# Gathering graph messages in tiles of 124 edges instead of 128

## The chip, the cores and the metric

The kernel runs on one core of one Trainium2 chip. The metric is the device time of the whole kernel in microseconds; lower is better. The kernel before takes 1381.88 us (median of two runs, 1380.68 and 1383.08).

Besides this time there is a profile of one execution. The profile's span, from its first to its last recorded instruction, is 1220.6 us. The device time is thus 161 us longer than the span. What lies in those 161 us the profile does not record.

## The reference

One layer of a graph network: each of 6250 nodes has 128 features, and 100000 edges of two types carry messages from a source node to a destination node. The edges come sorted by destination.

```
x    : [6250, 128] float32
src, dst, edge_type : [100000] int32, sorted by dst; type is 0 or 1

message(edge) = x[src] @ W_data.T + b_data          if type == 0
                x[src] @ W_control.T + b_control    otherwise
agg[n] = sum of message(edge) over the edges with dst == n
out    = layernorm(x + relu(agg + x @ W_self.T + b_self))
```

## The kernel before

Nodes are taken in 49 blocks of 128, and seven blocks make a group. The kernel has four stages.

1. It counts, for each block, how many destinations lie before it; that count is the place where the block's edges begin (line 96).
2. It multiplies all nodes with both message weights and stores the results in a table in DRAM, with row 2 * node + (type != 0) (lines 109 to 111).
3. For each block it loads a window of consecutive edges from the block's first one (line 123). KT = 18 tiles of P = 128 edges make a window of 2304 edges. An edge in the window that belongs to another block is to add nothing.
4. For each tile of a window, GpSimd starts an indirect DMA that gathers one table row of 512 bytes for each edge, each into a partition of its own (line 195). VectorE builds a one-hot matrix from the destinations (line 199). TensorE multiplies the two, which sums the messages by destination, and accumulates over the 18 tiles of the block (line 201). The residual and the layernorm follow.

The parts that matter here:

```
P = 128
KT = 18  # tiles of 128 edges in a block's window
WIN = KT * P
...
win = const.tile([P, NB, KT, 3], I32, name="win")
for b in range(NB):
    at = nc.values_load(first[0:1, b : b + 1], engines=(SP,), ...)
    nc.sync.dma_start(                                                   # line 123
        win[:, b, :, :], edges[ds(at, WIN), :].rearrange("(p k) c -> p k c", p=P)
    )
...
for g in range(NG):
    ...                             # idx, rel, low, inside of the whole group, on VectorE
    for j in range(GB):
        b = g * GB + j
        msg = deep.tile([P, KT, D], F32, name="msg")                     # 4 buffers
        hot = deep.tile([P, KT, P], F32, name="hot", bufs=3)
        agg = ps_a.tile([P, D], F32, name="agg")
        nc.tensor.matmul(agg, xt_sb[:, b, :], w_sb[:, 2 * D :], start=True, stop=False)
        for k in range(KT):
            nc.gpsimd.indirect_dma_start(                                # line 195
                out=msg[:, k, :], out_offset=None, in_=rows,
                in_offset=bass.IndirectOffsetOnAxis(ap=idx[:, j, k : k + 1], axis=0),
            )
            nc.vector.tensor_single_scalar(hot[:, k, :], slots, rel[:, j, k : k + 1],
                                           op=ALU.is_equal)              # line 199
            nc.tensor.matmul(agg, hot[:, k, :], msg[:, k, :],            # line 201
                             start=False, stop=k == KT - 1)
        residual(h[:, j, :], agg, b)
    norm_and_store(h, g)
```

At the end the kernel counts the edges that it matched. Only if one was missed does a loop over all edges do the sums again in any order. With the reference's inputs the fullest block has 2184 edges, fewer than the window holds, so the loop does not run.

Of the kernel before, what the change touches and what calls it, by code (L numbers as in the profile page):

```python
# [9 lines left out]
F32 = mybir.dt.float32  # L10
I32 = mybir.dt.int32
# [4 lines left out]
DRAM = bass.MemoryType.DRAM  # L16

P = 128
D = 128  # features
N = 6250  # nodes  # L20
E = 100000  # edges
NB = 49  # blocks of 128 nodes, the last one padded
NP = NB * P
GB = 7  # blocks in a group: one store, one set of norms
NG = NB // GB
KT = 18  # tiles of 128 edges in a block's window
WIN = KT * P
EC = 125  # edges are cut into 125 rows of 800
EPS = 1e-05


# [1 line left out]
def kernel(  # L33
    ctx: ExitStack,
    tc: tile.TileContext,
    x: bass.AP,  # [NP, D], zero rows behind N
    xt: bass.AP,  # [D, NP], its transpose
    edges: bass.AP,  # [E, 3]: source, destination, type
    w: bass.AP,  # [D, 3 * D]: data, control and self weights, transposed
    bias: bass.AP,  # [1, 3 * D]  # L40
    out: bass.AP,  # [N, D]
):
    """out = layernorm(x + relu(sum over in-edges of (W_type x_src + b_type) + W_self x + b_self))

    Both messages of each node go to a table in DRAM, at rows 2 * node + (type != 0). Edges come
    sorted by destination, so those of a block of 128 nodes lie behind one another: a window of
    WIN edges from the block's first one (found on the chip) is gathered from the table, 128 rows
    at a time, and summed by destination with one-hot matrices on the tensor engine. An edge
    outside its block matches no column there. The edges matched are counted; if any was missed
    (a block with more edges than its window, or edges in another order), a loop over all  # L50
    edges that takes them in any order does the sums again.
    """
    nc = tc.nc

    const = ctx.enter_context(tc.tile_pool(name="const", bufs=1))
    dram = ctx.enter_context(tc.tile_pool(name="dram", bufs=1, space=DRAM))
    work = ctx.enter_context(tc.tile_pool(name="work", bufs=2))
    deep = ctx.enter_context(tc.tile_pool(name="deep", bufs=4))
# [1 line left out]
    ps_a = ctx.enter_context(tc.tile_pool(name="ps_a", bufs=2, space=PSUM))  # L60
    ps_s = ctx.enter_context(tc.tile_pool(name="ps_s", bufs=1, space=PSUM))

# [1 line left out]
    e_all = const.tile([EC, E // EC, 3], I32, name="e_all")  # L64
    nc.gpsimd.dma_start(e_all, edges.rearrange("(p k) c -> p k c", p=EC))
    w_sb = const.tile([D, 3 * D], F32, name="w_sb")
# [9 lines left out]
    x_sb = const.tile([P, NB, D], F32, name="x_sb")  # L76
    x_rows = x.rearrange("(b p) f -> p b f", p=P)

# [1 line left out]
    ones = const.tile([P, 1], F32, name="ones")  # L80
    nc.vector.memset(ones, 1.0)
    slots = const.tile([P, P], F32, name="slots")
    nc.gpsimd.iota(slots, pattern=[[1, P]], base=0, channel_multiplier=0,
                   allow_small_or_imprecise_dtypes=True)
    base = const.tile([P, NB, KT], F32, name="base")
    nc.gpsimd.iota(base, pattern=[[P, NB], [0, KT]], base=0, channel_multiplier=0,
                   allow_small_or_imprecise_dtypes=True)

# [1 line left out]
    dst_f = const.tile([EC, E // EC], F32, name="dst_f")  # L90
    nc.vector.tensor_copy(dst_f, e_all[:, :, 1])  # L91
    before = const.tile([EC, NB], F32, name="before")
# [7 lines left out]
    first = const.tile([1, NB], I32, name="first")  # L100
    nc.vector.tensor_scalar_min(first, first_ps, float(E - WIN))

# [1 line left out]
    table = dram.tile([NP, 2 * D], F32, name="table")  # L104
    for g in range(NG):
        y = work.tile([P, GB, 2 * D], F32, name="y")
# [6 lines left out]
        )  # L113
    rows = table.rearrange("n (t f) -> (n t) f", t=2)

# [1 line left out]
    win = const.tile([P, NB, KT, 3], I32, name="win")  # L117
    for b in range(NB):
        at = nc.values_load(
            first[0:1, b : b + 1], engines=(SP,), min_val=0, max_val=E - WIN,  # L120
            skip_runtime_bounds_check_because="it counts edges and is held to E - WIN",
        )
        nc.sync.dma_start(
            win[:, b, :, :], edges[ds(at, WIN), :].rearrange("(p k) c -> p k c", p=P)
        )
    for g in range(NG):
        nc.scalar.dma_start(x_sb[:, g * GB : (g + 1) * GB, :], x_rows[:, g * GB : (g + 1) * GB, :])

    def table_rows(index, source, kind, shape):
        """index = 2 * source + (kind != 0)"""  # L130
        other = work.tile(shape, I32, name="other")
        nc.vector.tensor_single_scalar(other, kind, 0.0, op=ALU.not_equal)  # L132
        nc.vector.scalar_tensor_tensor(index, source, 2.0, other, op0=ALU.mult, op1=ALU.add)  # L133

    def residual(h, agg, b):
        """h = x + relu(agg + b_self)"""
        s = work.tile([P, D], F32, name="s")
        nc.vector.tensor_add(s, agg, bias_sb[:, 2 * D :])  # L138
        nc.vector.scalar_tensor_tensor(h, s, 0.0, x_sb[:, b, :], op0=ALU.max, op1=ALU.add)  # L139

    def norm_and_store(h, g):
        mv = work.tile([P, GB, 2], F32, name="mv")
        for j in range(GB):
            st = work.tile([P, 6], F32, name="st")
            nc.vector.bn_stats(st, h[:, j, :])  # L145
            nc.vector.bn_aggr(mv[:, j, :], st)  # L146
        # One step of Newton's method behind the table's square root: 1 / root is 2 / (s + v / s).
        v = work.tile([P, GB], F32, name="v")
        nc.vector.tensor_scalar_add(v, mv[:, :, 1], EPS)  # L149
        s0 = work.tile([P, GB], F32, name="s0")  # L150
        nc.scalar.activation(s0, v, AF.Sqrt)  # L151
        r0 = work.tile([P, GB], F32, name="r0")
        nc.vector.reciprocal(r0, s0)
        q = work.tile([P, GB], F32, name="q")
        nc.vector.tensor_mul(q, v, r0)
        nc.vector.tensor_add(q, q, s0)
        rstd = work.tile([P, GB], F32, name="rstd")
        nc.vector.reciprocal(rstd, q)
        nc.vector.tensor_scalar_mul(rstd, rstd, 2.0)
        o = work.tile([P, GB, D], F32, name="o")  # L160
        for j in range(GB):
            nc.vector.tensor_scalar(o[:, j, :], h[:, j, :], mv[:, j, 0:1], rstd[:, j : j + 1],  # L162
                                    op0=ALU.subtract, op1=ALU.mult)
        n0 = g * GB * P
        full = min(GB, (N - n0) // P)
        nc.sync.dma_start(
            out[n0 : n0 + full * P, :].rearrange("(b p) f -> p b f", p=P), o[:, :full, :]
        )
        if full < GB:
            n1 = n0 + full * P  # L170
            nc.sync.dma_start(out[n1:N, :], o[: N - n1, full, :])

# [1 line left out]
    counts = const.tile([P, NG], F32, name="counts")  # L174
    for g in range(NG):
        gs = slice(g * GB, (g + 1) * GB)
        shape = [P, GB, KT]
        idx = work.tile(shape, I32, name="idx")
        table_rows(idx, win[:, gs, :, 0], win[:, gs, :, 2], shape)
        rel = work.tile(shape, F32, name="rel")  # L180
        nc.vector.tensor_sub(rel, win[:, gs, :, 1], base[:, gs, :])  # L181
        low = work.tile(shape, F32, name="low")
        nc.vector.tensor_single_scalar(low, rel, float(P), op=ALU.is_lt)
        inside = work.tile(shape, F32, name="inside")
        nc.vector.scalar_tensor_tensor(inside, rel, 0.0, low, op0=ALU.is_ge, op1=ALU.mult,
                                       accum_out=counts[:, g : g + 1])
        h = work.tile([P, GB, D], F32, name="h")
        for j in range(GB):
            b = g * GB + j
            msg = deep.tile([P, KT, D], F32, name="msg")  # L190
            hot = deep.tile([P, KT, P], F32, name="hot", bufs=3)
            agg = ps_a.tile([P, D], F32, name="agg")
            nc.tensor.matmul(agg, xt_sb[:, b, :], w_sb[:, 2 * D :], start=True, stop=False)  # L193
            for k in range(KT):
                nc.gpsimd.indirect_dma_start(  # L195
                    out=msg[:, k, :], out_offset=None, in_=rows,
                    in_offset=bass.IndirectOffsetOnAxis(ap=idx[:, j, k : k + 1], axis=0),
                )
                nc.vector.tensor_single_scalar(hot[:, k, :], slots, rel[:, j, k : k + 1],  # L199
                                               op=ALU.is_equal)  # L200
                nc.tensor.matmul(agg, hot[:, k, :], msg[:, k, :], start=False, stop=k == KT - 1)  # L201
            residual(h[:, j, :], agg, b)
        norm_and_store(h, g)

# [1 line left out]
    total_ps = ps_s.tile([1, NG], F32, name="total_ps")  # L206
    nc.tensor.matmul(total_ps, ones, counts, start=True, stop=True)
    total_f = const.tile([1, 1], F32, name="total_f")
    nc.vector.tensor_reduce(total_f, total_ps, axis=mybir.AxisListType.X, op=ALU.add)
    total = const.tile([1, 1], I32, name="total")  # L210
# [1 line left out]
    matched = nc.values_load(total[0:1, 0:1])  # L212

    with tc.If(matched != E):
        # Rows behind N take what is not to be added: an edge whose destination an earlier edge of
        # its tile has already is in that edge's sum.
        sums = dram.tile([N + P, D], F32, name="sums")
        ident = const.tile([P, P], F32, name="ident")
        make_identity(nc, ident)
# [13 lines left out]
        with tc.For_i(0, E, EC) as i:  # L233
# [16 lines left out]
            n_again = work.tile([EC, 1], F32, name="n_again")  # L250
            nc.vector.scalar_tensor_tensor(again, same, 1.0, earlier[:EC, :EC], op0=ALU.mult,
                                           op1=ALU.mult, accum_out=n_again)
            # The destination, or a spare row where it came before.
            away = work.tile([EC, 1], F32, name="away")
            nc.vector.tensor_sub(away, spare[:EC], to)
            nc.vector.scalar_tensor_tensor(away, n_again, 0.0, away, op0=ALU.is_gt, op1=ALU.mult)
# [54 lines left out]
```

## Time and profile before

| What | Before |
|---|---|
| Device time, median | 1381.88 us |
| Span of the profile | 1220.6 us |
| GpSimd (POOL) busy | 843.7 us, 69% of the span |
| TensorE matmuls (PE) busy | 747.0 us, 61% |
| VectorE (DVE) busy | 305.0 us, 25% |
| DMA, mean rate | 63 GB/s |
| Indirect gathers | 882 = 49 blocks x 18 tiles |

The page gives, for each engine, the time it was busy, then the span in 40 slices of 30.5 us, then the DMA queues, then the chain of work that ended last, then the costliest groups of instructions. A group's row has its line in the kernel, its engine, its operation, the tiles that it writes and reads, how many there are, the total busy time and the mean of one in ns, and last the idle time of its engine just ahead of it with what ended that wait. The word "issue" stands for time in which an engine waited for nothing that the profile shows.

### The profile page before, as it was taken

How to read it: one execution, taken by the hardware profiler on the slowest of the kernel's cores; microseconds unless marked ns; L12 is line 12 of the kernel's file. 1: busy time of each engine (PE TensorE's matmuls, PEld its weight loads, DVE VectorE, ACT ScalarE, POOL GpSimd, SP SyncE). 2: the span in 40 equal slices, each digit the busy share in tenths (PEclk: the TensorE clock that was granted, in tenths of full speed). 3: DMA queues.
4: the chain of work that ended last, by engine and by line, in shares of the span. 5: the costliest groups of instructions: out<-in, count | busy, mean ns of one | idle time of the engine just before them, and what ended most of it. 6: DMA issues, size and time to landing. Idle time of an engine off the chain costs nothing.

```text
span 1220.6 us, 6620 instructions
## 1 busy us (share of the span) xinstructions
PE 747.0 (61%) x1964; PEld 478.7 (39%) x1964; DVE 305.0 (25%) x1362; ACT 2.7 (0%) x8; POOL 843.7 (69%) x889
## 2 busy tenths in 40 slices
PE   1094666666666666666666666666666666666664
PEld 0042444444444344444444444444444444444442
DVE  4982211221212312212213113113122112212101
ACT  0000000000000000000000000000000000000000
POOL 0005777777777777777777777777777777777774
PEclk9995555555555555555555555555555555555555
DMA  8063121122212211121222212222122211221121
GB/s 263 0 200 95 52 54 52 52 67 54 52 52 52 69 52 52 52 54 52 67 54 53 52 52 67 54 52 53 52 67 54 52 52 52 68 53 52 52 54 49
DMA packets 55893, 77.32 MB, mean 63 GB/s; under 512 B 21669, under 2 KB 40719, under 8 KB 55727
## 3 DMA queue, kind: packets, MB, share of 16 engines
q0 software_dynamic: 28368, 59.06, 18.6%
q1 hardware_dynamic: 14716, 8.16, 2.5%
q10 hardware_dynamic: 12768, 9.63, 2.4%
q8 instruction: 16, 0.26, 0.1%
q14 instruction: 25, 0.20, 0.1%
HBM read 67.17 MB, written 9.62 MB: 63 GB/s over the span
## 4 chain that ended last, share of the span: by engine, by line
POOL 63%; issue 23%; DMA 5%; DVE 5%; PE 2%; POOLq 0%; SPq 0%; DVEq 0%; ACT 0%; ACTq 0%
POOL msg L195 63%; DMA msg<-table,idx 4%; DVE less L96 4%; PE y_ps L109 2%; DMA xt_sb<-in_xt 1%; DVE hot L199 1%; DVE y L110 1%; PE agg L201 0%; DVE o L162 0%; POOLq L307 0%; SPq L67 0%; SPq L69 0%; POOLq L195 0%; PE first_ps L99 0%; DVE other L132 0%
## 5 line engine op out<-in xcount | busy, mean ns | idle before, releaser
L195 POOL DMA_INDIRECT msg<-table,idx x882 | 840.9, 953 | 362.6 <-issue 259.5
L201 PE MATMUL agg<-msg,hot 128*128 128x128 f32 x1764 | 695.2, 500 | 403.0 <-DMA msg<-table,idx 400.7
L201 PEld LDWEIGHTS agg<-msg,hot 128*128 128x128 f32 x1764 | 441.0, 311 | 656.5 <-DMA msg<-table,idx 656.2
L138 DVE TENSOR_TENSOR s<-agg,bias_sb 128x128 f32<-128x128 f32 x49 | 14.3, 292 | 790.4 <-PE agg L201 790.4
L199 DVE TENSOR_SCALAR hot<-slots,rel 128x128 f32<-128x128 f32 x882 | 189.0, 292 | 0.0
L96 DVE TENSOR_SCALAR_CACHE_REDUCE less<-dst_f 125x800 f32<-125x800 f32 x48 | 43.6, 980 | 0.0
L109 PE MATMUL y_ps<-w_sb,xt_sb 128*128 128x256 f32 x98 | 31.4, 449 | 18.5 <-DMA xt_sb<-in_xt 16.8
L193 PE MATMUL agg<-w_sb,xt_sb 128*128 128x128 f32 x98 | 31.2, 423 | 0.0
L109 PEld LDWEIGHTS y_ps<-w_sb,xt_sb 128*128 128x128 f32 x98 | 16.5, 207 | 31.9 <-issue 16.8
L193 PEld LDWEIGHTS agg<-w_sb,xt_sb 128*128 128x128 f32 x98 | 27.0, 333 | 0.6 <-DVE s L138 0.3
L99 PE MATMUL first_ps<-before,ones 125*1 125x49 f32 x2 | 0.3, 260 | 41.5 <-DVE less L96 41.5
L133 DVE SCALAR_TENSOR_TENSOR idx<-win,other 128x126 int32<-128x126 int32 x7 | 2.3, 324 | 88.0 <-DMA msg<-table,idx 88.0
L110 DVE TENSOR_TENSOR y<-y_ps,bias_sb 128x256 f32<-128x256 f32 x49 | 20.5, 424 | 5.0 <-PE y_ps L109 3.8
L99 PEld LDWEIGHTS first_ps<-before,ones 125*1 125x1 f32 x2 | 0.1, 80 | 41.8 <-DVE less L96 41.8
L139 DVE SCALAR_TENSOR_TENSOR h<-s,x_sb 128x128 f32<-128x128 f32 x49 | 14.5, 295 | 0.1
L145 DVE BATCH_NORM_STATS2 st<-h 128x6 f32<-128x128 f32 x49 | 13.7, 280 | 0.1
L162 DVE TENSOR_SCALAR o<-h,mv,rstd 128x128 f32<-128x128 f32 x49 | 13.5, 363 | 0.0
L146 DVE BATCH_NORM_AGGREGATE mv<-st 128x2 f32<-128x6 f32 x49 | 8.6, 176 | 0.9
L91 DVE CAST dst_f<-e_all 125x800 f32<-125x800 int32 x1 | 0.7, 693 | 15.5 <-DMA e_all<-in_edges 15.5
L151 ACT ACTIVATE s<-v 128x7 f32<-128x7 f32 x7 | 1.5, 208 | 1115.5 <-DVE v L149 1115.5
L96 DVE DVE_READ_ACCUMULATOR less<-dst_f 125x1 f32 x48 | 3.9, 82 | 0.0
L181 DVE TENSOR_TENSOR rel<-win,base 128x126 f32<-128x126 int32 x7 | 2.1, 305 | 0.0
(25 smaller groups left out, 19.2 us busy)
## 6 DMA issues: line engine op xcount, KB each, us to landing
msg<-table,idx POOLq DMA_INDIRECT x882, 2.5
table<-y ACTq DMA_DIRECT2D x7, 896.0 KB, 4.2
x_sb<-in_x ACTq DMA_DIRECT2D x7, 448.0 KB, 14.6
xt_sb<-in_xt SPq DMA_DIRECT2D x7, 448.0 KB, 10.4
out<-o SPq DMA_DIRECT2D x6, 448.0 KB, 3.0
win<-in_edges SPq DMA_DIRECT2D x49, 27.0 KB, 1.9
e_all<-in_edges POOLq DMA_DIRECT2D x1, 1171.9 KB, 15.2
out<-o SPq DMA_DIRECT2D x1, 384.0 KB, 3.4
```

What stands on the lines that cost most here:

```text
L96: nc.vector.tensor_scalar(less, dst_f, float(b * P), None, op0=ALU.is_lt, op1=ALU.add, accum_out=before[:, b : b + 1])
L109: nc.tensor.matmul(y_ps, xt_sb[:, g * GB + j, :], w_sb[:, : 2 * D], start=True, stop=True)
L110: nc.vector.tensor_add(y[:, j, :], y_ps, bias_sb[:, : 2 * D])
L138: nc.vector.tensor_add(s, agg, bias_sb[:, 2 * D :])
L139: nc.vector.scalar_tensor_tensor(h, s, 0.0, x_sb[:, b, :], op0=ALU.max, op1=ALU.add)
L145: nc.vector.bn_stats(st, h[:, j, :])
L146: nc.vector.bn_aggr(mv[:, j, :], st)
L162: nc.vector.tensor_scalar(o[:, j, :], h[:, j, :], mv[:, j, 0:1], rstd[:, j : j + 1], op0=ALU.subtract, op1=ALU.mult)
L193: nc.tensor.matmul(agg, xt_sb[:, b, :], w_sb[:, 2 * D :], start=True, stop=False)
L195: nc.gpsimd.indirect_dma_start(out=msg[:, k, :], out_offset=None, in_=rows, in_offset=bass.IndirectOffsetOnAxis(ap=idx[:, j, k : k + 1], a ...
L199: nc.vector.tensor_single_scalar(hot[:, k, :], slots, rel[:, j, k : k + 1], op=ALU.is_equal)
L201: nc.tensor.matmul(agg, hot[:, k, :], msg[:, k, :], start=False, stop=k == KT - 1)
```

## The change

A tile has R = 124 edges instead of 128. There are still 18 tiles to a window, so a window has 2232 edges instead of 2304, and the tiles `win`, `idx`, `rel`, `low`, `inside`, `msg` and `hot` have 124 partitions instead of 128. The sums of a block still go to 128 destinations. The fullest block's 2184 edges still fit into a window.

It is for the way in which an indirect gather is shared among the DMA engines[...].

The comments are also taken out of the file; line numbers in the part that matters are kept within one of the old ones. The core of the diff:

```diff
-KT = 18  # tiles of 128 edges in a block's window
-WIN = KT * P
+KT = 18
+R = 124
+WIN = KT * R
...
-    win = const.tile([P, NB, KT, 3], I32, name="win")
+    win = const.tile([R, NB, KT, 3], I32, name="win")
...
-            win[:, b, :, :], edges[ds(at, WIN), :].rearrange("(p k) c -> p k c", p=P)
+            win[:, b, :, :], edges[ds(at, WIN), :].rearrange("(p k) c -> p k c", p=R)
...
-        shape = [P, GB, KT]
+        shape = [R, GB, KT]
...
-        nc.vector.tensor_sub(rel, win[:, gs, :, 1], base[:, gs, :])
+        nc.vector.tensor_sub(rel, win[:, gs, :, 1], base[:R, gs, :])
...
-                                       accum_out=counts[:, g : g + 1])
+                                       accum_out=counts[:R, g : g + 1])
...
-            msg = deep.tile([P, KT, D], F32, name="msg")
-            hot = deep.tile([P, KT, P], F32, name="hot", bufs=3)
+            msg = deep.tile([R, KT, D], F32, name="msg")
+            hot = deep.tile([R, KT, P], F32, name="hot", bufs=3)
...
-                nc.vector.tensor_single_scalar(hot[:, k, :], slots, rel[:, j, k : k + 1],
+                nc.vector.tensor_single_scalar(hot[:, k, :], slots[:R], rel[:, j, k : k + 1],
                                                op=ALU.is_equal)
...
-    nc.tensor.matmul(total_ps, ones, counts, start=True, stop=True)
+    nc.tensor.matmul(total_ps, ones[:R], counts[:R], start=True, stop=True)
```

## The prediction

> **What bounds the kernel now.** I start with the page's chain of work that ended last, because it says which engine sets the end. The columns are shares of the span.
>
> ```profile
> POOL 63%; issue 23%; DMA 5%; DVE 5%; PE 2%; POOLq 0%; SPq 0%; DVEq 0%; ACT 0%; ACTq 0%
> POOL msg L195 63%; DMA msg<-table,idx 4%; DVE less L96 4%; PE y_ps L109 2%; DMA xt_sb<-in_xt 1%; DVE hot L199 1%; DVE y L110 1%; PE agg L201 0%; DVE o L162 0%; POOLq L307 0%; SPq L67 0%; SPq L69 0%; POOLq L195 0%; PE first_ps L99 0%; DVE other L132 0%
> ```
>
> Work of GpSimd on the gathers and the "issue" time between them are 86% of the chain. Next come the costliest groups of instructions.
>
> ```profile
> L195 POOL DMA_INDIRECT msg<-table,idx x882 | 840.9, 953 | 362.6 <-issue 259.5
> L201 PE MATMUL agg<-msg,hot 128*128 128x128 f32 x1764 | 695.2, 500 | 403.0 <-DMA msg<-table,idx 400.7
> L201 PEld LDWEIGHTS agg<-msg,hot 128*128 128x128 f32 x1764 | 441.0, 311 | 656.5 <-DMA msg<-table,idx 656.2
> L199 DVE TENSOR_SCALAR hot<-slots,rel 128x128 f32<-128x128 f32 x882 | 189.0, 292 | 0.0
> ```
>
> One gather occupies GpSimd for 953 ns. TensorE, the second busiest, waits 401 us in total for gathered rows: it follows GpSimd. To see whether GpSimd itself waits for anything I look at the timeline of the middle of the run (start, duration, what, and in brackets the idle time ahead and what ended it).
>
> ```profile
> 635.30 0.95 POOL L195 DMA_INDIRECT msg<-table,idx  x1 [0.30 <-issue]
> 635.39 0.50 PEld L201 LDWEIGHTS agg<-msg,hot 128*128 128x128 f32 x2 [0.81 <-DMA msg<-table,idx]
> 635.40 0.79 PE L201 MATMUL agg<-msg,hot 128*128 128x128 f32 x2 [0.52 <-DMA msg<-table,idx]
> 636.55 0.95 POOL L195 DMA_INDIRECT msg<-table,idx  x1 [0.30 <-issue]
> ```
>
> GpSimd works 0.95 us, pauses 0.30 us, and begins the next gather 1.25 us after the last. No semaphore ends the pause. The gathers run from 98 us (the first start that the trace gives for the line) to 1207.6 us (the last one's end): 1109.5 us for 882, or 1.258 us each. They are 91% of the span, and the rest of the program follows their pace: everything depends on how long GpSimd takes over one gather.
>
> Last, the DMA side, from the page's queues (packets, MB, share of 16 engines' span) and its list of issues (count, KB, us to landing).
>
> ```profile
> q0 software_dynamic: 28368, 59.06, 18.6%
> ...
> msg<-table,idx POOLq DMA_INDIRECT x882, 2.5
> ```
>
> The queue that GpSimd feeds keeps 16 engines busy for only 18.6% of the span. The DMA engines don't bound the kernel.
>
> [...] 28368 packets less the 144 that I leave to the other GpSimd load make 28224 = 882 x 32, which is 16 packets of data and 16 completions to a gather. [...] Here 8 rows x 512 bytes are just 4096, [...] which fits the 32. [...] the bar is 0.95 us, the landing is at 2.5 us. [...]
>
> **The change part by part.**
>
> *Fewer rows to a gather.* 128 to 124, or 3.1% fewer. If all 953 ns were spent row by row, this saves 953 x 4/128 = 30 ns, and over 882 gathers 26 us. This is the upper bound of this part.
>
> *Fewer shares.* Twelve of the 16 data shares go; the 16 completions stay. If all 953 ns went to the 32 pieces and nothing to rows, 12/32 of it would go: 357 ns, 315 us in all. This is an upper bound too. If instead the work goes by packets, then 31 rows in packets of 8 are 4 packets to an engine and again 16 to a gather, and nothing is saved.
>
> *The split that I choose.* The only other DMA that GpSimd starts is the plain load of the edges, 125 rows, 698 ns by the group of line 65. It has nearly as many rows and no indices. I therefore put the difference, 953 - 698 = 255 ns, down to the indices, row by row. The 698 ns I divide in three equal parts, for want of anything in the profile that divides them: 233 ns fixed, 233 by rows, 233 by shares and completions. Rows: (255 + 233) x 4/128 = 15 ns. Shares: 233 x 12/32 = 87 ns. Sum 102 ns to a gather, 882 x 102 ns = 90 us, all on the path that sets the end. This is an estimate; the equal thirds are a choice.
>
> *The 0.30 us pause.* It is between any two gathers, and I take it as unchanged.
>
> *Data on four engines.* Queue 0 was busy 0.186 x 16 x 1220.6 = 3632 engine-us; over 882 gathers at most 4.1 to a gather or 0.257 us to an engine for 8 rows and a completion, so at most 0.032 us for a row. 31 rows would then take 1.0 us on one engine, and a gather lands 0.74 us later, at some 3.2 us. [...] Hidden, because four buffers of 18 gathers lie ahead of TensorE. Only the very last gather's delay, under 1 us, reaches the end.
>
> *TensorE and VectorE.* Matrices with 124 rows instead of 128 stream the same 128 columns, so no saving in time is counted. Two pairs of matmuls back to back took 1.31 us at 626.02 us in the timeline, one alone 0.80: a further pair costs 0.51 us, well under the coming pace of 1.15 us. VectorE needs 0.21 us (189.0 us / 882) for each one-hot matrix. Neither becomes the bound.
>
> *The window loads on SP.* [...] The first group's indices start at 71.8 us, while the first gather waits until 98.1 us for the table; later groups have far more slack. At most 1 us is lost.
>
> *The sum.* 1381.9 - 90 + about 2 = 1294 us. Since one rival below costs time and one gives only the rows' part, I put the point at 1300 us.
>
> **The rivals.**
>
> *Rows or packets are all that counts.* [...] Then only up to 26 us go: 1356 to 1378 us. For it: the number of packets may stay at 32, and the plain 125-row load is not dramatically cheaper. Against it: nothing in the trace; the kernel has no other gather of another size.
>
> *Shares are nearly everything.* The saving nears 315 us: 1070 to 1180 us. [...] Against it: the completions for all engines remain, and the 0.30 us pause is untouched.
>
> *A slower path for the odd size.* 128 rows on 16 engines may be the well-trodden case, and 31 rows to an engine, with partial packets, may take more work per row. If a gather takes 10% longer, 95 ns x 882 = 84 us are lost: 1466 us. Nothing in the profile speaks for or against it.
>
> *The same four engines every time.* [...] four engines must take 1.0 us of rows every 1.15 us: 87% busy. The landing would grow and GpSimd might wait for space. The pace would be held near 1.0 to 1.25 us, so the gain would shrink rather than turn to a loss.
>
> **Range and chances.** The row and packet rival gives the upper part, the shares rival the lower one. I take 1160 to 1405 us for 8 in 10: it holds everything from three fifths of the full shares saving or so, (1381.9 - 1160) / (315 + 26) = 65%, up to a loss of 23 us. The limits of 2% are 1354 and 1410 us. Faster by over 2% gets 0.60, for it needs only 28 us or 32 ns a gather, which rows alone just miss and any real cost of shares brings. Within 2% gets 0.24, slower 0.16 for the odd-size path.
>
> **What would show it.** The group of line 195: its mean falls from 953 to about 850 ns if the thirds are right, to 923 or more if rows alone count, below 700 if shares are nearly everything, and rises over 953 on a slower path. The pause ahead of it stays 0.30 us. Queue 0's packets per gather tell how 31 rows are cut: 32 if in packets of 8, 20 if one packet holds an engine's share. The landing goes from 2.5 to about 3.2 us[...]. If GpSimd's wait for gathers in flight appears in place of "issue", the engines have become the bound. What would make the prediction wrong is above all the division into thirds. A second risk lies in the 161 us between span and device time, which I take as fixed: were they a stretch of the same gathers, the saving would be an eighth larger.

## The result, and the profile after

The changed kernel takes **1522.88 us** (median of 1522.2 and 1523.56) against 1381.88 us: ratio **1.102**, 95% interval 1.0988 to 1.1052. Beside the kernel before on another chip, where that one takes 1220.12 us, the ratio is **1.252** (1.2496 to 1.2538); the changed kernel hardly differs there, 1527.24 us. Why there are two ratios is taken up with the experiments. In both the change costs time, and it was predicted to save some, with 1300 us as the point.

The profile's span is 1521.5 us after 1220.6. First the chain of work that ended last, in shares of the span by engine.

```profile
POOL 65%; issue 19%; DMA 9%; DVE 3%; SPq 2%; PE 2%; POOLq 0%; DVEq 0%; ACT 0%; ACTq 0%
```

The chain is made of the same things as before, GpSimd's gathers and the pauses between them: 84% where it was 86%. No new wait has taken their place. Next the costliest groups (busy us, mean ns of one, idle time ahead and what ended it).

```profile
L196 POOL DMA_INDIRECT msg<-table,idx x882 | 1137.0, 1289 | 366.6 <-issue 256.4
L202 PE MATMUL agg<-msg,hot 124*128 124x128 f32 x1764 | 700.7, 501 | 696.1 <-DMA msg<-table,idx 695.9
...
L200 DVE TENSOR_SCALAR hot<-slots,rel 124x128 f32<-124x128 f32 x882 | 235.0, 398 | 0.0
```

One gather now takes 1289 ns of GpSimd instead of 953, though it fetches four rows fewer. The pauses are as they were (256.4 us in total after 259.5). TensorE computes as long as before, 501 ns a matmul after 500, and waits longer for rows: 696 us instead of 401. The gathers' busy time alone has grown by 1137.0 - 840.9 = 296 us, and the span by 301.

The DMA queue that GpSimd feeds (packets, MB, share of 16 engines' span) shows more packets:

```profile
q0 software_dynamic: 70704, 58.57, 16.7%
```

(70704 - 144) / 882 = **80 packets a gather**, where there were 32, with fewer bytes moved. The packet records of the trace, sorted by size, tell what they are:

| Bytes of a packet | Number in the trace | A gather | What it fits |
|---|---|---|---|
| 4096 | 10584 | 12 | 8 rows of 512 bytes: 3 in each of 4 lists |
| 3584 | 3528 | 4 | 7 rows: 1 in each of 4 lists |
| 32 | 31752 | 36 | 8 pieces of 4 bytes: 3 in each of 12 lists |
| 28 | 10584 | 12 | 7 pieces of 4 bytes: 1 in each of 12 lists |
| 4 | 14131 | 16 | 16 completions |

The packets of 4 bytes are taken for completions because the trace has as many of them, over all queues, as semaphore events that come from DMAs: 14810. A packet's record has its queue and size and not its DMA engine. The counts fit sixteen lists of 31 entries, each cut into packets of 8, 8, 8 and 7: four lists of rows, as I had assumed of 124 = 4 x 31, and twelve of pieces of 4 bytes. These pieces, 12 x 31 = 372 to a gather, are called **fillers** here; what they are for the trace does not say. The trace of the kernel before has 14112 packets of 4096 bytes, 16 to a gather, and none of 32 or 28 bytes: sixteen lists of 8 rows. So there are still sixteen lists, and by these counts every list has become 31 entries long instead of 8.

### The profile page after: what moved, and what is told of

It is laid out like the page before. It is cut to its first block, busy times and chain, and to the rows that moved or that the text cites. A ratio compares the mean times of both kernels' runs of the same rounds, so it can differ in the third digit from the quotient of the medians.

```text
span 1521.5 us, 6620 instructions
## 1 busy us (share of the span) xinstructions
PE 753.5 (50%) x1964; PEld 479.7 (32%) x1964; DVE 354.4 (23%) x1362; ACT 2.7 (0%) x8; POOL 1139.9 (75%) x889
## 3 DMA queue, kind: packets, MB, share of 16 engines
q0 software_dynamic: 70704, 58.57, 16.7%
## 4 chain that ended last, share of the span: by engine, by line
POOL 65%; issue 19%; DMA 9%; DVE 3%; SPq 2%; PE 2%; POOLq 0%; DVEq 0%; ACT 0%; ACTq 0%
POOL msg L196 65%; DMA msg<-table,idx 7%; DVE less L97 3%; PE agg L202 2%; SPq L120 1%; DMA xt_sb<-in_xt 1%; SPq L124 1%; DMA win<-in_edges 0%; POOLq L308 0%; DVE o L163 0%; PE y_ps L110 0%; DVE y L111 0%; SPq L70 0%; SPq L68 0%; DVE st L146 0%
## 5 line engine op out<-in xcount | busy, mean ns | idle before, releaser
L196 POOL DMA_INDIRECT msg<-table,idx x882 | 1137.0, 1289 | 366.6 <-issue 256.4
L202 PE MATMUL agg<-msg,hot 124*128 124x128 f32 x1764 | 700.7, 501 | 696.1 <-DMA msg<-table,idx 695.9
L202 PEld LDWEIGHTS agg<-msg,hot 124*128 124x128 f32 x1764 | 441.2, 310 | 955.5 <-DMA msg<-table,idx 955.4
L200 DVE TENSOR_SCALAR hot<-slots,rel 124x128 f32<-124x128 f32 x882 | 235.0, 398 | 0.0
L163 DVE TENSOR_SCALAR o<-h,mv,rstd 128x128 f32<-128x128 f32 x49 | 14.6, 419 | 0.0
L147 DVE BATCH_NORM_AGGREGATE mv<-st 128x2 f32<-128x6 f32 x49 | 12.3, 250 | 0.9
L157 DVE TENSOR_TENSOR q<-q,s 128x7 f32<-128x7 f32 x7 | 3.3, 466 | 0.0
```

Source lines behind the costliest of these rows:

```text
L196: nc.gpsimd.indirect_dma_start(out=msg[:, k, :], out_offset=None, in_=rows, in_offset=bass.IndirectOffsetOnAxis(ap=idx[:, j, k : k + 1], a ...
L200: nc.vector.tensor_single_scalar(hot[:, k, :], slots[:R], rel[:, j, k : k + 1], op=ALU.is_equal)
```

## The experiments

**The theories.** Theory A: a gather costs GpSimd a fixed part and a step for each row of the longest list; 124 rows make 31 steps, 128 rows make 8. Theory B: any gather with rows in fewer than 16 lists pays a fixed penalty. Theory C: the packets of a list count, 4 instead of 1. Theory E: the number of fillers counts. How other numbers of rows are divided is an assumption of mine: into as many lists of equal length as possible, up to 16. The expectations say "engine" for what is a list here. Packets were counted for 128, 124 and 127 rows alone, so for the rest the time of a gather is the test.

**The kernel before again (no edit).**

> The kernel before, run again on the same chip as the next three, to have its profile and its device time side by side: the first profile had a span of 1220.6 us where the device time was 1381.88 us, while the changed kernel has 1521.5 and 1522.88 us. If the gap is part of the program outside the recorded span, the span is again about 161 us shorter than the device time. If instead the gathers run at two different paces, 953 ns in one execution and about 181 ns more, (1381.88 - 1220.6) / 882 gathers, in another, then span and device time of one and the same execution agree within a few us, as they do for the changed kernel.

Measured: 1221.69 us in the median of 20 executions, and 1221.64 us for the kernel before in 23 others beside it. The span of the profiled one is 1220.2 us at a device time of 1222.37. So span and device time differ by 2 us in one and the same execution. The 161 us that the prediction took for a fixed part of the program are none.

**126, 125 and 120 rows.** The edits, on the changed kernel:

```diff
-R = 124
+R = 126        # or 125; or 120 with KT = 19
```

> Tiles of 126 rows, 18 to a window: [...] Theory A, rows to an engine: [...] a gather costs a fixed part and a step for each row to an engine. From 953 ns at 8 rows and 1289 ns at 31 rows: 14.6 ns a step, 836 ns fixed; 9 rows give 968 ns. Theory B, a fixed penalty for every gather that does not use all 16 engines: 1289 ns. Theory C, a cost for each packet to an engine, (1289 - 953) / 3 = 112 ns for each beyond the first: 2 packets, 1065 ns. In every theory the pause of 0.30 us stays.

> Tiles of 125 rows, 18 to a window: [...] Theory A, rows to an engine: 836 + 25 x 14.6 = 1201 ns. Theory B, a fixed penalty: 1289 ns. Theory C, packets to an engine: 4 packets as with 124 rows, 1289 ns. [...] 16 x 5 = 80 packets a gather on GpSimd's queue, as with 124.

> Tiles of 120 rows, 19 to a window, so that 2280 edges still cover the fullest block: 931 gathers instead of 882. [...] Theory A: 953 ns, as with 128 rows, because the rows to an engine are the same. Theory B: 1289 ns. Theory C: 953 ns. Under A and C the time rises over the kernel before by 49 gathers of 1.26 us, 62 us of span. 32 packets a gather[...].

Measured, from the costliest groups of the three profiles, in this order:

```profile
L196 POOL DMA_INDIRECT msg<-table,idx x882 | 879.7, 997 | 366.0 <-issue 255.7
```
```profile
L196 POOL DMA_INDIRECT msg<-table,idx x882 | 1063.4, 1206 | 365.8 <-issue 261.5
```
```profile
L196 POOL DMA_INDIRECT msg<-table,idx x931 | 917.3, 985 | 383.1 <-issue 270.4
```

| Rows | Lists x rows, assumed | Gather, ns | A | B | C | Time, us | Ratio to the kernel before |
|---|---|---|---|---|---|---|---|
| 126 | 14 x 9 | 997 | 968 | 1289 | 1065 | 1264.90 | 1.0354 (1.0337 to 1.0372) |
| 125 | 5 x 25 | 1206 | 1201 | 1289 | 1289 | 1450.07 | 1.1869 (1.1849 to 1.1889) |
| 120 | 15 x 8 | 985 | 953 | 1289 | 953 | 1318.67 | 1.0792 (1.0774 to 1.0810) |

B falls: a gather of 126 rows takes 997 ns and not 1289. C falls too: 125 and 124 rows would both have four packets to a list and differ by 83 ns, and 126 rows with two packets take hardly more than 120 with one. A is near everywhere, but 29 to 32 ns low at 126 and 120. A small fixed part for rows in fewer than 16 lists has to be added. With it 120 rows cost 49 more gathers of 1.29 us, 63 us, and 882 x 32 ns, 28 us: 91 of the 97 us measured. The first gather also starts 4.8 us later (103.9 after 99.1 us).

**Nineteen sizes side by side.** The edit, on the kernel before, 12 gathers of each size n ahead of its end:

```diff
+    got = deep.tile([P, KT, D], F32, name="msg")
+    for k in range(12):
+        nc.gpsimd.indirect_dma_start(out=got[:n, k, :], out_offset=None, in_=rows,
+            in_offset=bass.IndirectOffsetOnAxis(ap=idx[:n, 0, k : k + 1], axis=0))
```

> The kernel before with 228 more gathers ahead of its end, 12 of each of 19 sizes, into a buffer that nothing reads. Theory A, a step for each row of the engine that has most, whoever fills the others, with about 35 ns more when fewer than 16 engines have rows: 16, 32, 48, 64, 80, 96, 112, 128 rows (1 to 8 to an engine) rise by 13.5 ns from size to size, from 850 to 944 ns; 31, 62, 93 and 124 rows (31 rows each to 1, 2, 3, 4 engines) all take the same 1287 ns; 15 rows 885, 120 rows 979, 126 rows 992, 100 rows (10 each to 10 engines) 1006, 125 rows 1208, 61 rows on one engine 1695, 127 rows on one engine 2586 ns. Theory E, the fillers are what costs (0.85 ns each) and rows cost nothing: all sizes that use 16 engines take 944 ns alike; 31 rows take 82 ns more than 124, because their fillers are 465 against 372. The rows theory of the prediction, a cost for each row gathered: 31 rows are far cheaper than 124.

The groups by line, GpSimd alone; each size has a line of its own. These ten are, from above and divided as assumed, 127 rows in one list, 61 in one, then 124, 93, 62 and 31 rows, all in lists of 31, then 120 rows in 15 lists, 128 in 16, 15 in 15 and 16 in 16.

```profile
L262 POOL DMA_INDIRECT msg<-table,idx x12 | 30.5, 2542 | 3.7 <-issue 3.7
L253 POOL DMA_INDIRECT msg<-table,idx x12 | 19.9, 1658 | 3.7 <-issue 3.7
L241 POOL DMA_INDIRECT msg<-table,idx x12 | 15.4, 1284 | 3.7 <-issue 3.7
L247 POOL DMA_INDIRECT msg<-table,idx x12 | 15.3, 1272 | 3.7 <-issue 3.7
L250 POOL DMA_INDIRECT msg<-table,idx x12 | 15.1, 1260 | 3.7 <-issue 3.7
L256 POOL DMA_INDIRECT msg<-table,idx x12 | 15.1, 1259 | 3.7 <-issue 3.7
...
L235 POOL DMA_INDIRECT msg<-table,idx x12 | 11.7, 972 | 3.7 <-issue 3.7
L208 POOL DMA_INDIRECT msg<-table,idx x12 | 11.3, 943 | 3.7 <-issue 3.7
...
L259 POOL DMA_INDIRECT msg<-table,idx x12 | 10.4, 865 | 3.7 <-issue 3.7
...
L229 POOL DMA_INDIRECT msg<-table,idx x12 | 10.1, 841 | 3.7 <-issue 3.7
```

This is the run that tells the theories apart. A gather of 31 rows takes as long as one of 124, within 25 ns, as theory A has it with 31 steps for both. So the rows gathered cost nearly nothing, (1284 - 1259) / 93 = 0.27 ns each, and what counts is the longest list. From 31 to 127 rows in one list a step is (2542 - 1259) / 96 = 13.4 ns; in 16 lists, from 1 to 8 rows in each, (943 - 841) / 7 = 14.6 ns. Theory E falls twice: 31 rows, with more fillers by its own count (465 after 372), are not dearer than 124, and from 16 to 128 rows, sizes without a filler by that count, the time rises all the same. The nine sizes not shown, the multiples of 16 between and 100, 125 and 126 rows, follow the assumed division too: the first take 863 to 926 ns, the last three, with lists of 10, 25 and 9 rows, 992, 1191 and 980 ns. The extra for rows in fewer than 16 lists shows in neighbours with equal lists: 15 rows 865 ns against 16 rows 841, 120 rows 972 against 128 rows 943. It is 24 to 29 ns.

The 341 ns more of 124 rows (1284 - 943) are thus 29 ns extra for rows in fewer than 16 lists (972 - 943) and 312 ns for 23 steps more (1284 - 972), 13.6 ns each. One part of theory A stays open. With the fillers all sixteen lists are equally long by the packet counts, so a step more is sixteen entries more. Whether a step is work on sixteen lists side by side, or on one entry after another at some 13.6 / 16 = 0.85 ns each, these runs don't tell.

**All rows in one list.** The edit is R = 127.

> Tiles of 127 rows: [...] Theory A: 871 + 127 x 13.5 = 2586 ns a gather, with the pause 2.89 us, span 112 + 882 x 2.89 = 2660 us. Packets: 16 engines x (16 of data or filler + 1 completion) = 272 a gather. Theory B, a fixed penalty for fewer than 16 engines, as with 124 rows: 1289 ns, span 1520 us. The engine's own work, 16 packets of 4096 bytes at 0.16 us, is 2.5 us, so a gather lands at 5 us or more; if the engines are taken in turn this stays hidden, and if it were always the same engine it would set a pace of about 2.5 us, still under GpSimd's 2.89.

Measured: 2657.48 us, ratio 2.178 (2.1736 to 2.1824). The group and the queue:

```profile
q0 software_dynamic: 240048, 65.33, 15.4%
...
L196 POOL DMA_INDIRECT msg<-table,idx x882 | 2243.3, 2543 | 392.0 <-issue 386.5
```

The time came within 3 us of theory A's, but in part by luck: the gather is 43 ns shorter, 38 us in all, while the first one starts at 127.6 us, some 28 us later than in the kernel before (99.1). (240048 - 144) / 882 is 272 packets, as expected. The data packets of 4096 bytes took 0.23 us each in the mean of the packet records. Fifteen of them and one of 3584 bytes, one after another, are 3.6 us, more than the 2.85 us from one gather to the next; yet GpSimd never waited for a transfer, and a third of the data packets start while another is still under way. A gather lands 7.8 us after its issue in the median, so several are in flight at once; on which DMA engines their packets go is not shown.

**The changed kernel again, and one part of it undone.** In the second kernel the windows, indices, one-hot matrices and matmuls keep 124 rows, and only the gather goes back to 128; nothing reads the last four rows.

> The changed kernel again, beside the kernel before on one chip. The kernel before took 1221.6 us in 43 runs beside the last experiments, in keeping with its profile (1220.6) and not with its first two times (1381.88). If those two times are the odd ones, the changed kernel takes 1522 us again and the ratio is about 1.246: (1289 - 953) ns x 882 = 296 us more. If the pace of a gather changes from chip to chip, both kernels' times differ from 1221.6 and 1522.

Measured: 1527.24 us against 1220.12, ratio 1.2517 (1.2496 to 1.2538), the gather 1293 ns. As expected, this is a chip of the first kind, on which the kernel before takes 1220 to 1222 us; on the second kind it takes 1376 to 1384.

```diff
-        idx = work.tile(shape, I32, name="idx")
-        table_rows(idx, ...)
+        idx = work.tile([P, GB, KT], I32, name="idx")
+        nc.vector.memset(idx, 0)
+        table_rows(idx[:R], ...)
...
-            msg = deep.tile([R, KT, D], F32, name="msg")
+            msg = deep.tile([P, KT, D], F32, name="msg")
...
-                nc.tensor.matmul(agg, hot[:, k, :], msg[:, k, :], ...)
+                nc.tensor.matmul(agg, hot[:, k, :], msg[:R, k, :], ...)
```

> The changed kernel with one part undone: windows, indices, one-hot matrices and matmuls keep their 124 rows, but each gather fetches 128 rows, the last four of which (row 0 of the table) nothing reads. Only the way the gather is shared changes back, to 16 engines with 8 rows each. Theory A: 944 to 953 ns a gather again and 1222 us, within 5 us of the kernel before, so that the whole 307 us between 1220 and 1527 lie in the shape of the gather. Rival: a part of the loss comes from the other uses of 124 rows (window loads on four engines, VectorE and TensorE on 124 partitions); then a part of it remains, and the time lies clearly over 1225 us.

Measured: 1379.44 us, ratio 1.002, but on a chip where the kernel before takes 1376.43. The gathers are at 949 ns again, as theory A has it:

```profile
L197 POOL DMA_INDIRECT msg<-table,idx x882 | 837.1, 949 | 503.7 <-issue 252.0
```

Yet 882 x 1.25 us and the 112 us around them make 1215. The timeline of GpSimd shows where the rest is (start, duration, what, idle time ahead and what ended it):

```profile
627.75 0.94 POOL L197 DMA_INDIRECT msg<-table,idx  x1 [0.30 <-issue]
629.00 0.94 POOL L197 DMA_INDIRECT msg<-table,idx  x1 [0.30 <-issue]
...
636.15 0.94 POOL L197 DMA_INDIRECT msg<-table,idx  x1 [6.21 <-remote]
```

GpSimd stands still for 6 us. By the gathers' start times this happens 22 times, always at the first gather of a block, where it needs one of the four message buffers, and costs 138 us together. On this chip the buffers are not emptied in time, and GpSimd runs out of them.

> The last kernel again. There its gathers took 949 ns as theory A has it, but on that chip both it and the kernel before took 1376 to 1379 us instead of 1221, with TensorE's work in bursts 51 us apart and GpSimd waiting some 6 us in each: something other than the gathers set the pace, so the times could not separate the theories. On a chip where the kernel before takes about 1221 us this one takes 1222 to 1226 us under theory A; under the rival (a part of the loss in the other uses of 124 rows) clearly more. On a chip like the last one, about 1379 us again.

> The changed kernel a third time. On a chip where the kernel before takes 1221 us: 1523 to 1527 us, ratio 1.25. On a chip where the kernel before takes about 1376 us because TensorE sets the pace at (1376 - 112) / 1862 = 0.68 us a matmul of the main stage, or 1.43 us a tile, the changed kernel's GpSimd, at 1.59 us a tile, is the slower of the two and still takes about 1525 us: ratio 1.10 to 1.11, as in the first comparison. The rival, that such a chip is slower in everything by 13%, gives 1720 us there and a ratio of 1.25.

> The kernel with windows of two blocks again. On a chip where the kernel before takes 1221 us: 1166 us, ratio 0.955. On a chip where TensorE sets the pace at 0.68 us a matmul it has 3206 of them in the main stage instead of 1862, and takes 112 + 3206 x 0.68 = 2290 us, ratio 1.66; then it beats the kernel before only where TensorE is free to keep up.

The first two of these three, on one chip of that kind, against 1376.43 us for the kernel before: gathers of 128 rows 1378.91 us, ratio 1.0022 (1.0014 to 1.0029); the changed kernel 1522.62 us, ratio 1.1068 (1.1042 to 1.1093). The latter is the ratio of the first comparison. It is smaller because the kernel before is held up there, not because the change costs less: the changed kernel's gathers come 1.59 us apart and leave its consumers more time, GpSimd has no stall over 1 us in its trace, and it runs at the same pace on both kinds. Undoing the gather alone takes back 143.7 of the 146.2 us that the change costs on this chip.

> The changed kernel with gathers of 128 rows, once more. Where the kernel before takes about 1221 us: 1222 to 1226 us if the whole loss lies in how a gather is shared (theory A), clearly more if a part lies in the other uses of 124 rows. Where the kernel before takes about 1376 us: 1379 us, which tells nothing new.

> The changed kernel with gathers of 128 rows, for a chip on which the kernel before takes about 1221 us: 1222 to 1226 us if the whole loss lies in how a gather is shared (theory A), clearly more if a part lies in the other uses of 124 rows. Where the kernel before takes about 1376 us: about 1379 us, as three times already.

Both met that kind again and repeat the result: 1379.78 against 1376.38 us and 1386.24 against 1383.61, ratios 1.0023 and 1.0018. The time of this kernel where the kernel before takes 1221 us has therefore not been measured; the length of its gathers has.

**What holds the kernel before on those chips.** Every second matmul of the tiles is left out, and with it the sums of half of the edges:

```diff
-                nc.tensor.matmul(agg, hot[:, k, :], msg[:, k, :], ...)
+                if k % 2 == 1:
+                    nc.tensor.matmul(agg, hot[:, k, :], msg[:, k, :], ...)
```

> The kernel before with every second matmul of the tiles left out (the sums of half of the edges are missing from its output; all gathers and one-hot matrices remain). Where the kernel before takes about 1221 us, GpSimd sets the pace and nothing changes: 1221 us, ratio 1.00. Where it takes about 1376 us: if TensorE sets the pace there, the time falls to about 1221 us, ratio 0.887; if something else there makes GpSimd or the transfers wait, it stays at 1376 us.

Measured: 1359.08 us against 1376.38, ratio 0.9886 (0.9867 to 0.9904). This is near the second outcome: half of TensorE's tile work gone brings 17 us of some 155. So, against what I had thought, the amount of matmuls is not what sets the pace there. The trace of the kernel with gathers of 128 rows (1379.44 us) agrees: TensorE is busy for 24% of its span and idle for some 35 us at a time. From 601.6 to 636.3 us, for one, it does nothing, while the gathers' data and completion packets keep coming, 16 of each to a gather, until GpSimd stalls. The cause stays open. The trace puts the waits down to "remote", a releaser that it can't name. It holds only 2618 of the DMA completions' semaphore events, where that of the kernel before on the first kind of chip holds 15394, so its waits can't be read.

**Fewer gathers of the cheap size.** If a gather of 128 rows is as cheap as it gets, only fewer gathers help. Here three windows of two blocks and one of one block serve a group. The buffers change with it: three of 34 tiles for messages instead of four of 18, and twelve single one-hot matrices instead of three sets of 18.

```diff
+KT2 = 34  # tiles in the window of two blocks
+UNITS = ((0, 2, 0, KT2), (2, 2, KT2, KT2), (4, 2, 2 * KT2, KT2), (6, 1, 3 * KT2, KT))
...
+                nc.vector.tensor_single_scalar(hot[:, : nb * P], slots[:, : nb * P],
+                                               rel[:, c0 + k : c0 + k + 1], op=ALU.is_equal)
+                for i in range(nb):
+                    nc.tensor.matmul(aggs[i], hot[:, i * P : (i + 1) * P], msg[:, k, :],
+                                     start=False, stop=k == kt - 1)
```

> Fewer gathers of the cheap size. In each group of seven blocks, three windows of two blocks (34 tiles of 128 rows each) and one window of one block (18) replace seven windows of 18: 120 gathers instead of 126, 840 instead of 882 in all. Each tile of a two-block window has a one-hot matrix of 256 columns and two matmuls, one for each block. Theory A: a gather of 128 rows stays at 953 ns plus 0.30 us of pause, so 42 gathers fewer save 42 x 1.255 = 53 us: 1169 us, ratio 0.957. Rival: TensorE needs 2 x 0.51 = 1.02 us for a tile, near GpSimd's 1.25; if its matmuls run slower than that, TensorE becomes the bound and the gain is lost.

Measured: 1165.58 us against 1220.12, ratio **0.955** (0.9534 to 0.9566), the 53 us of theory A almost exactly. The groups:

```profile
L206 POOL DMA_INDIRECT msg<-table,idx x840 | 795.5, 947 | 349.1 <-issue 344.9
L214 PE MATMUL agg<-msg,hot 128*128 128x128 f32 x3108 | 828.4, 416 | 220.6 <-DMA msg<-table,idx 170.4
```

On a chip of the second kind it is the other way round: 1472.18 us against 1376.43, ratio 1.0692 (1.0659 to 1.0724). The 2290 us that I expected from a fixed pace of each matmul were far off, which agrees with the open cause above. So this version beats both kernels on one kind of chip and on the other only the changed one.

## Why the prediction was wrong

**The bound was right.** GpSimd's gathers set the pace before and after, the pause stayed at 0.30 us, and TensorE and VectorE did not become the bound. Of the 305.2 us between the spans 1220.2 and 1525.4 us, on the two chips of the first kind, 301.0 are the gathers' busy time (839.7 to 1140.7).

**The step that failed is "Fewer shares".** It let twelve of sixteen data shares go and counted 87 ns saved. That 124 rows leave four shares was an estimate of mine, and the packet counts fit it; but the other twelve lists do not go, they hold 372 fillers. And the split had no term for the length of a share, which costs some 13.5 ns a row. The prediction's "a row" was a row of the gather; the one that counts is a row of the longest list. In its place: 23 more steps, +312 ns, and +29 ns for rows in fewer than 16 lists, 341 ns in all instead of -102.

**"Fewer rows" was mis-sized too.** 488 ns were put down to rows, 15 ns of them saved. With 0.27 ns a row, four rows are 1 ns. The 255 ns between the plain load and the gather, which I took as a cost of indices, row by row, must lie elsewhere.

**The packet test was well chosen and answered outside its two cases.** 32 or 20 packets were expected; 80 came, and the extra 48, of 32 or 28 bytes, are the fillers.

**Of the rivals,** the slower path for the odd size had the direction right, but sized it at a tenth where the gather took 35% longer (1289 after 953 ns), and gave it a chance of 0.16. It named shares of 31 rows, which the packet counts fit, but with more work for each row; the runs show more steps at the same cost of a step, 13.4 to 14.6 ns. The signs of the same four engines every time did not come: GpSimd has no wait for a transfer in the changed kernel, and the landing is 3.7 us. Which engine takes a packet was not shown. The sixteen completions to a gather stayed (14131 packets of 4 bytes).

**Smaller terms.** The landing was predicted at 3.2 us and is 3.7 on the chip where the trace gives it. The first gather begins 3.2 us later (102.3 after 99.1 us in the spans compared), more than the 1 us allowed for the window loads. The last part of the table is issued at 96.6 us instead of 93.9; with 127 rows it is issued at 120.4 us, and the first gather begins at 127.6. What holds it up was not tested. The 161 us taken as fixed were not part of the program; the first profile and the first two times are, by the later runs, from chips of the two kinds.

## What to carry to other kernels

In these runs an indirect gather cost GpSimd by its longest list and not by its rows: 943 ns for 128 rows in lists of 8, but 1284 ns for 124 and 1259 ns for 31 rows in lists of 31, and 2542 ns for 127 in one list. The multiples of 16 took 841 to 943 ns, and 128 the least for each row: keep the number of rows a multiple of 16, and best at 128. This is shown for rows of 512 bytes and up to 128 of them. Four rows fewer turned 8 steps into 31, and one row fewer into 127; pad to the good shape and leave the extra rows unread. When a profile's span and the device time are far apart, settle why before adding them up: here they came from executions of different pace, and the same change costs 25% against one and 10 to 11% against the other.

## What was not expected of the hardware

By the packet counts a gather of 124 rows has 372 fillers of 4 bytes beside its rows, where one of 128 has none. Some of VectorE's instructions took longer beside longer lists: a one-hot matrix took 293 ns in the mean with 8 rows to a list, 344 with 25, 398 with 31 and 788 with 127, while the median stayed at 276 to 280. With 127 rows, 280 of the 882 took over 0.4 us, 1.9 us in the mean, and each of these ended within 0.13 us after the end of a gather. The 124 rows of the matrices are not the reason: beside gathers of 128 rows the mean was 295 again. It cost nothing here, since VectorE is far from the bound (busy for 23% of the changed kernel's span). The kernel before took 1220 to 1222 us on two chips and 1376 to 1384 us on four, with gathers of the same length.
